# Layer 3's weighted sums in the scores' PSUM banks, earlier degrees, and the loads of layer 0 in a new order

## The chip, the cores and the metric

The kernel runs on one core of a Trainium2 chip, in one launch. The metric is the device time of the whole launch in microseconds. Before the change it is 3578.55 us, the median of 3 runs (3575.83 to 3585.26). The profiled execution has a span of 3568.9 us and a mean granted TensorE clock of 0.977.

## What is computed

There are 64 graphs of 256 nodes with 256 features, and a dense 256 x 256 adjacency matrix for each, all in fp32. Four layers follow each other, and each is `x = layernorm(x + layer(x, adj))`:

```
# layer 0: a recurrence over the nodes i = 0..255 (h starts as x)
x_par = sum_j (adj[j, i] / deg[i]) * h[j]
r, z  = sigmoid(x_i @ W_ioux.T + b + x_par @ W_iouh.T + b)
hc    = tanh(x_i @ W_coux.T + b + (x_par * r) @ W_couh.T + b)
h[i]  = z * x_par + (1 - z) * hc
# layer 1: relu(norm_adj @ (x @ W.T + b)), norm_adj = adj / sqrt(deg_i deg_j)
# layer 2: one attention head of width 256, mask = adj, relu on q, k, v and output
# layer 3: attention with 8 heads of width 32, masked where adj <= 0, output projection
```

Node i of the recurrence reads states of earlier nodes and, for the later nodes, x itself. So its 256 steps run one after the other, with all 64 graphs side by side. Layers 1 to 3 work on each graph by itself.

## The kernel before

**Setup of layer 0** (`_recurrence`, up to L714). The weights of the cell come first: four loads through `_load_wT` (L44), turned by TensorE transposes into WxT and WhT; then the biases, cut into three bf16 parts (L56), and small masks ("window", L149). A pool of their own holds these, and it is closed before the next one opens.

Then comes the part of the parents' sum that needs only x (L185 to L209): in eight groups of GB = 8 graphs, adj (A, two transfers from SyncE's queue) and x (Xs, two from ScalarE's) are loaded into two buffers each, GpSimd cuts A to a triangle (L195), TensorE multiplies (L172), ScalarE and VectorE copy the PSUM banks in turn (L208), and the sums go to Us in DRAM (L179).

After that follow, one after the other, the degrees of the first block of T = 32 nodes (`degrees(0)`, L267: four pieces of rows, each loaded and then reduced; then `dinv`), the adjacency block S, the first sums ACC from Us (L298), the masked block An (L464), and the first x (xq).

**The steps.** One step: the parents' sum xp is turned (L597), multiplied with WhT for r and z (L590), rx is turned and multiplied for the candidate, and VectorE makes the new state (L631). ScalarE copies the state to `hs` (L633), and two transfers put it into a ring of 64 nodes in SBUF, Hw (L640, `into_ring`). `flush` (L619) writes rows of the ring to Hd in DRAM: 32 at a time in each block, the last 16 after the last step (L855). The order of instructions in the steps is written by hand (`manual_schedule`). Loads that may wait go through `load_later`, which puts them in a queue by rank; two of them are begun in each of the first four steps of eight (L820).

**Layers 1 to 3** (`_layers`). When the recurrence is done, the weights, rows and columns of the three layers are loaded from ScalarE's queue (L877 to L884), W1 is turned, and a product of the values' bias with Wo is added to a bias row (L899). Then 64 graphs go through a pipeline written out by hand: `ROUND` (L1194) lists steps such as `B.qk2.0`; the letter says how many rounds ago the graph entered (L is the youngest, then A, B, C; E has layer 3's end), and each round begins with the loads of one new graph (L981).

PSUM has four banks under the tag "mm" (`bank`, L930), which every product and transposition takes in turn, and four banks "sc0" to "sc3" for the scores of layer 3 (L1126). The scores of one half of the heads (`s3`) fill the four "sc" banks; VectorE adds the mask (L1141), ScalarE takes the exponential (L1142), and GpSimd adds the two halves of the keys (p3s, L1144). `o3` (L1148) takes two "mm" banks, one for each half of the heads, and puts there the weighted sums (L1164) and the sums of the exponentials (L1155). `d3` (L1175) divides. `degrees_a` and `degrees_b` (L1001, L1012) make the inverse root of the degrees, `dis`, which `adT` (L1016) uses when it copies the turned adjacency.

Of the kernel before, what the change touches and what calls it, by code (L numbers as in the profile page):

```python
# [19 lines left out]
P = 128  # L20
# [50 lines left out]
def _recurrence(tc, ident, Hd, x, adj, W_ioux, b_ioux, W_iouh, b_iouh, W_coux, b_coux, W_couh, b_couh):  # L71
# [31 lines left out]
    with ExitStack() as ctx:  # L103
# [20 lines left out]
        with tc.tile_pool(name="r_setup", bufs=1) as tmp, tc.tile_pool(  # L124
            name="r_setup_ps", bufs=2, space=bass.MemoryType.PSUM
        ) as tps:
            for WT, wi, wc, s in ((WxT, W_ioux, W_coux, "x"), (WhT, W_iouh, W_couh, "h")):
                _load_wT(nc, tmp, tps, wi, ident, lambda c: WT[:, :, c % 2, c // 2 * 2, :], "i" + s)
                _load_wT(nc, tmp, tps, wc, ident, lambda c: WT[:, :, c, 1, :], "c" + s)
            bx, bh = (tmp.tile([1, 2, 3, P], F32, name=f"bias_{s}") for s in "xh")  # L130
            for t, bi, bc in ((bx, b_ioux, b_coux), (bh, b_iouh, b_couh)):
                for g in range(2):
                    nc.scalar.dma_start(
                        t[:, :, 2 * g, :],
                        bi[g * D:(g + 1) * D].rearrange("(c d) -> c d", c=2).unsqueeze(0),
                    )
                nc.scalar.dma_start(t[:, :, 1, :], bc.rearrange("(c d) -> c d", c=2).unsqueeze(0))
            nc.vector.tensor_add(bx, bx, bh)
            _split_bf16(nc, tmp, bias3, bx, "bias")

            span = tmp.tile([W, T // U, U], F32, name="span")
            nc.gpsimd.memset(span, 1.0)
            nc.gpsimd.affine_select(
                out=span, in_=span, pattern=[[U, T // U], [0, U]], compare_op=ALU.is_ge,
                fill=0.0, base=W - T // 2 - LAG - 1, channel_multiplier=-1,
            )
            for w in range(2):  # L149
                first = (w * T - W + T // 2) % W  # L150
                for lo, hi, at in ring(first, first + W):
                    for g in range(2):
                        nc.sync.dma_start(
                            window[w][g * W + at:g * W + at + hi - lo],
                            span[lo - first:hi - first].rearrange("p a u -> p (a u)"),
                        )
# [26 lines left out]


        with tc.tile_pool(name="r_first", bufs=2) as tmp, tc.tile_pool(  # L185
            name="r_first_ps", bufs=4, space=bass.MemoryType.PSUM
        ) as tps:
            for g in range(0, B, GB):
                A = tmp.tile([P, 2, GB, P], F32, tag="A", name=f"xA_{g}")
                Xs = tmp.tile([P, 2, GB, D], F32, tag="X", name=f"xX_{g}")  # L190
                for jc in range(2):
                    rows = slice(jc * P, (jc + 1) * P)
                    nc.sync.dma_start(A[:, jc], adj[g:g + GB, rows, 0:P].rearrange("b j i -> j b i"))
                    nc.scalar.dma_start(Xs[:, jc], x[g:g + GB, rows, :].rearrange("b j d -> j b d"))
                nc.gpsimd.tensor_mul(  # L195
                    A[:, 0], A[:, 0], tri.unsqueeze(1).to_broadcast([P, GB, P])
                )
                for n in range(0, GB, 4):
                    ub = tmp.tile([P, 4, D], F32, tag="ub", name=f"xu_{g}_{n}")
                    for e in range(0, 4, 2):  # L200
                        pb = tps.tile([P, 2, D], F32, tag="x", name=f"xp_{g}_{n}_{e}")
                        for q in range(2):
                            b = n + e + q
                            x_product(
                                pb, q, [A[:, jc, b, :] for jc in range(2)],
                                [Xs[:, jc, b, :] for jc in range(2)],
                            )
                        (nc.vector.tensor_copy if e else nc.scalar.copy)(ub[:, e:e + 2, :], pb)  # L208
                    x_out(0, g + n, ub)  # L209

        blk = ctx.enter_context(tc.tile_pool(name="r_blk", bufs=2))
        stream = ctx.enter_context(tc.tile_pool(name="r_stream", bufs=2))
        work = ctx.enter_context(tc.tile_pool(name="r_work", bufs=2))
        ps = ctx.enter_context(tc.tile_pool(name="r_ps", bufs=1, space=bass.MemoryType.PSUM))
# [24 lines left out]
        def load_later(out, in_, rank):  # L239

            begun = []

            def f(n):
                nc.sync.dma_start(out, in_)
                begun.append(n)

            loads.append((rank, f))
            loads.sort(key=lambda e: e[0])
            return begun
# [17 lines left out]
        def degrees(k):  # L267
# [16 lines left out]
            nc.vector.tensor_scalar(zero, deg, 0.0, None, ALU.is_equal)  # L284
            nc.vector.tensor_add(deg, deg, zero)
            nc.vector.reciprocal(deg, deg)
            nc.vector.tensor_scalar(zero, zero, -1.0, 1.0, ALU.mult, ALU.add)
            nc.vector.tensor_mul(deg, deg, zero)
            yield
            for h in range(2):  # L290
                at = k * T + h * HT
                for c in range(2):
                    nc.sync.dma_start(dinv[c * B:(c + 1) * B, at:at + HT], deg[h * B:(h + 1) * B])
# [69 lines left out]
        def early_load(e, got=[]):  # L363
# [5 lines left out]
            Hs = stream.tile([P, GB, D], F32, tag="Hs", name=f"Hs_{k}_{lo}_{t}", bufs=4)  # L369
# [267 lines left out]
        def into_ring():  # L637
            n, hs = ring_in.pop(0)
            for o in range(2):
                nc.sync.dma_start(Hw[n % W::W, :, o * P:(o + 1) * P], hs[o * B:(o + 1) * B])  # L640
# [19 lines left out]
        for _ in degrees(0):  # L660
            pass
        tables[0]["S"], double = load_S(0)
        double()
        tables[0]["Sd"] = chain_S(0)
        tables[0]["An"] = late_load(0)
        for a in range(3):
            sums_in(a)

        xq = {0: load_x(0)}
# [3 lines left out]
        xq[1] = load_x(1)  # L673
# [35 lines left out]
        for now in range(N):  # L709
# [9 lines left out]
            if n:  # L719
# [13 lines left out]
                if p > 3:  # L733
# [104 lines left out]
            if i == 24:  # L838
                flush(n - 8 - T, n - 8)
            early_ahead(n)  # L840
# [14 lines left out]
        flush(N - T // 2, N)  # L855


def _layers(tc, ident, Hd, Yd, x, adj, w1, b1, l2, l3, out):
# [8 lines left out]
    nc = tc.nc  # L867
    B, N, D = x.shape
# [5 lines left out]
    with ExitStack() as ctx:  # L874
        const = ctx.enter_context(tc.tile_pool(name="l_const", bufs=1))
        W1T = const.tile([P, 2, D], F32, name="W1T")
        W2 = {n: _load_w(nc, const, l2["W" + n], f"W2{n}") for n in "qkvo"}  # L877
        W3 = {n: _load_w(nc, const, l3["W" + n], f"W3{n}") for n in "qkvo"}
        b1_r = _load_row(nc, const, b1, "b1_r")
        b2_r = _load_row(nc, const, l2["bo"], "b2o_r")  # L880
        b3_r = _load_row(nc, const, l3["bo"], "b3o_r")
        cols = const.tile([P, 6, 2], F32, name="b_cols")
        for s, b in enumerate((l2["bq"], l2["bk"], l3["bq"], l3["bk"], l3["bv"], l2["bv"])):
            _load_col(nc, cols[:, s, :], b)  # L884
# [5 lines left out]
        with tc.tile_pool(name="l_setup", bufs=1) as tmp, tc.tile_pool(  # L890
            name="l_setup_ps", bufs=2, space=bass.MemoryType.PSUM
        ) as tps:
            _load_wT(nc, tmp, tps, w1, ident, lambda c: W1T[:, :, c * P:(c + 1) * P], "w1")

            bv = tmp.tile([P, 2, P], F32, name="bv3")
            nc.vector.tensor_copy(bv, cols[:, 4, :].unsqueeze(2).to_broadcast([P, 2, P]))
            pb = tps.tile([P, D], F32, tag="wt", name="bv3_ps")
            for k in range(2):
                nc.tensor.matmul(pb, bv[:, k, :], W3["o"][:, k, :], start=(k == 0), stop=(k == 1))  # L899
            nc.vector.tensor_add(b3_r, b3_r, pb)  # L900
# [5 lines left out]
        ctx.enter_context(tc.manual_schedule())  # L906
# [23 lines left out]
        def bank(name, shape=(P, 2, D)):  # L930
            return ps.tile(list(shape), F32, tag="mm", name=name, bufs=4)

# [40 lines left out]
        class Graph:  # L973
# [7 lines left out]
            def load(self):  # L981
                b = self.b
                self.y = io.tile([P, 2, D], F32, tag="y", name=f"y_{b}", bufs=7)
                nc.sync.dma_start(self.y, Hd[:, b, :].rearrange("(c p) d -> p c d", p=P))
# [3 lines left out]
                nc.sync.dma_start(self.ad, adj[b].rearrange("(c p) m -> p c m", p=P))  # L988

# [158 lines left out]
            def o3(self):  # L1148


                self.o_ps = [bank(f"o3_{self.b}_{hc}") for hc in range(2)]
# [43 lines left out]
            A.xT.1 B.xT.2 E.o3 E.d3.0 C.norm_b.2 E.d3.1 B.qk2.0  # L1195
            A.t B.qk2.1 B.v2 L.residual_0 B.masks
            E.f3 C.xT.3 A.g C.bias_3 L.norm_a.0
            C.qk3.0 C.qk3.1 E.norm_a.3 A.norm_a.1 L.norm_b.0 B.s2 B.exp2
            C.s3.0 C.v3 B.w2 L.degrees_a
            B.pT2 E.norm_b.3 E.store A.norm_b.1 C.s3.1 B.f2 L.degrees_b  # L1200
# [192 lines left out]
```

## Time and profile before

| Part of the trace | from to (us) | what is there |
|---|---|---|
| weights, masks | 0 to 21 | transposes of the cell's weights; DMA share 0.52, then 0.03 |
| x part of the sums | 21 to 122.6 | 8 groups; the last store to Us has landed at 122.6 |
| degrees, first loads | 122.6 to 152.8 | four loads and reductions of rows in turn, then dinv |
| 256 steps | 152.8 to 1563.1 | the last state is copied at 1562.83 to 1563.10 |
| passage to the layers | 1563.1 to 1595.2 | the last flush, then weights, then the first graph's loads |
| layers 1 to 3 | 1595.2 to 3569 | a new graph about every 30.0 us |

Over the whole span TensorE is busy 3223.1 us (90%), VectorE 2465.2 (69%), ScalarE 1900.3 (53%) and GpSimd 1874.5 (53%). These shares are means over stages with different limits, so the stages have to be read one by one: in a table of windows the columns are the busy time of TensorE, of its weight loads, of VectorE, ScalarE and GpSimd with the number of instructions, then the granted TensorE clock, the share of the 16 DMA engines, and GB/s. In the timeline and in the lists of groups, L1164 is line 1164 of the kernel, `a<-b` is output and inputs, and the bracket at the end has the idle time of the engine before the instruction and what ended it. TensorE's rows "x16" are instructions: an fp32 matmul is several of them.

### The profile page before, as it was taken

What the parts mean: (1) busy time and instruction counts of PE and PEld (TensorE: products, weight loads), DVE (VectorE), ACT (ScalarE), POOL (GpSimd) and SP (SyncE); (2) the same over time, 40 slices, a digit from 0 to 9 for tenths busy, and PEclk for the clock granted to TensorE, in tenths of its full rate; (3) what the DMA queues carried; (4) which work ended last, traced back from release to release, by engine and by line L of the source; (5) the groups of instructions that cost most, each with busy time, mean ns of one, the idle gap of its engine ahead of it and who ended that gap; (6) DMA issues with size and microseconds to landing.
All of it is one profiled execution on the core that took longest, in us unless ns stands there. A gap on an engine that the chain in (4) does not pass through costs nothing.

```text
span 3568.9 us, 80419 instructions
## 1 busy us (share of the span) xinstructions
PE 3223.1 (90%) x29350; PEld 2318.4 (65%) x29350; DVE 2465.2 (69%) x7052; ACT 1900.3 (53%) x5026; POOL 1874.5 (53%) x2181
## 2 busy tenths in 40 slices
PE   5599999999989898858999999999999999999998
PEld 4455555555555555536777777777777777777775
DVE  2366767767667777735777777777777777777776
ACT  0155545545445454424666666666666666666664
POOL 2266677767667778723444444444444444444443
PEclk9799999999999999978999999999999999999999
DMA  8846566787876564140111111111111111111100
GB/s 281 224 132 144 162 174 152 162 190 201 201 191 166 154 152 120 58 116 18 45 45 45 45 45 45 45 45 45 45 45 45 45 45 45 45 43 45 45 27 22
DMA packets 389637, 348.43 MB, mean 98 GB/s; under 512 B 107244, under 2 KB 355192, under 8 KB 384120
## 3 DMA queue, kind: packets, MB, share of 16 engines
q1 hardware_dynamic: 367280, 323.84, 34.0%
q10 hardware_dynamic: 21960, 19.41, 1.6%
q8 instruction: 235, 3.85, 0.4%
q14 instruction: 162, 1.33, 0.1%
HBM read 224.01 MB, written 99.61 MB: 91 GB/s over the span
## 4 chain that ended last, share of the span: by engine, by line
PE 61%; DVE 14%; DMA 6%; issue 6%; POOL 6%; ACT 5%; SPq 2%; ACTq 0%; DVEq 0%; POOLq 0%
PE mm L948 13%; PE rc L590 4%; DVE p L1141 4%; PE s L1132 4%; PE rc L582 3%; PE mm_g L948 3%; PE mm_t L948 3%; PE mm_3f L948 3%; PE mm_3v L948 3%; PE mm_2s L948 3%; PE mm_2v L948 3%; PE late L506 3%; DVE ACC L615 3%; PE mm_2w L948 3%; POOL ACC L651 2%
## 5 line engine op out<-in xcount | busy, mean ns | idle before, releaser
L615 DVE SCALAR_TENSOR_TENSOR ACC<-keep,S,ACC 128x128 f32<-128x128 f32 x1712 | 504.8, 345 | 187.4 <-ACT hs L633 170.0
L1144 POOL TENSOR_TENSOR p3s<-p 128x256 f32<-128x256 f32 x512 | 387.8, 788 | 329.6 <-ACT p L1142 329.3
L925 ACT ACTIVATE y<-y,shift,rstd 128x256 f32<-128x256 f32 x512 | 273.4, 593 | 303.9 <-DVE shift L923 259.9
L1044 POOL TENSOR_TENSOR y<-y,g 128x512 f32<-128x512 f32 x64 | 81.1, 1267 | 601.1 <-issue 590.2
L651 POOL TENSOR_TENSOR ACC<-ACC,far 128x384 f32<-128x384 f32 (+1 forms) x313 | 371.3, 1186 | 24.6
L582 PE MATMUL rc<-WxT,xqT 128*64 128x256 f32 x2048 | 326.3, 397 | 6.1 <-ACT lb L232 1.7
L1141 DVE TENSOR_TENSOR p<-s,neg 128x512 f32<-128x512 f32 x512 | 317.7, 683 | 10.9 <-PE s L1132 8.8
L755 POOL TENSOR_TENSOR ready<-ACC,dinv 128x128 f32<-128x128 f32 x255 | 101.9, 400 | 391.3 <-DVE ACC L615 372.4
L647 POOL TENSOR_TENSOR far<-hs,S 128x384 f32<-128x384 f32 (+1 forms) x313 | 304.3, 972 | 4.7
L1142 ACT ACTIVATE p<-p 128x512 f32<-128x512 f32 x512 | 294.6, 624 | 2.6 <-DVE p L1141 1.6
L913 DVE BATCH_NORM_STATS2 st<-y 128x6 f32<-128x256 f32 x512 | 209.0, 408 | 95.0 <-POOL y L1044 90.2
L917 POOL TENSOR_TENSOR rstd<-rstd,mhalf 128x2 f32<-128x2 f32 x256 | 173.6, 695 | 125.7 <-DVE rstd L916 122.2
L1178 DVE RECIPROCAL rT<-o 128x256 f32<-128x256 f32 x128 | 223.8, 1748 | 0.3 <-PE o L1155 0.2
L599 ACT COPY xpT<-xpT_ps 128x128 f32<-128x128 f32 x256 | 68.3, 267 | 254.9 <-PE xpT_ps L597 254.9
L1164 PE MATMUL o<-p,v 128*32 128x256 f32 x2048 | 138.4, 382 | 70.8 <-ACT xT L1030 70.8
L590 PE MATMUL rc<-WhT,xpT 128*64 128x128 f32 x2048 | 170.7, 288 | 28.8 <-ACT xpT L599 28.6
L590 PEld LDWEIGHTS rc<-WhT,xpT 128*64 128x64 f32 x2048 | 108.1, 137 | 118.6 <-ACT xpT L599 84.1
L1187 DVE TENSOR_TENSOR y<-y,mm_3f 128x512 f32<-128x512 f32 x64 | 44.0, 688 | 187.9 <-PE mm_3f L948 187.9
L582 PE MATMUL z_ps<-WxT,xqT 128*64 128x128 f32 x2048 | 170.0, 287 | 0.0
L1107 ACT ACTIVATE qk<-mm,b_cols 128x256 f32<-128x256 f32 x256 | 107.5, 471 | 115.9 <-PE mm L948 115.9
L506 PE MATMUL late<-Hw,An 64*32 64x256 f32 x3840 | 154.9, 389 | 9.3 <-issue 4.4
L815 DVE TENSOR_TENSOR zcc<-zc,rc 128x128 f32<-128x128 f32 x256 | 72.7, 284 | 130.0 <-ACT rc L813 129.3
(168 smaller groups left out, 8004.6 us busy)
## 6 DMA issues: line engine op xcount, KB each, us to landing
xX<-in_x_dram ACTq DMA_DIRECT2D x16, 1024.0 KB
Us<-xu SPq DMA_DIRECT2D x64, 256.0 KB
rows<-in_adj_dram SPq DMA_DIRECT2D x64, 256.0 KB
ACC<-Us SPq DMA_DIRECT2D x32, 512.0 KB
xq<-in_x_dram SPq DMA_DIRECT2D x64, 256.0 KB
Hw<-hs SPq DMA_DIRECT2D x512, 32.0 KB
Es<-eu SPq DMA_DIRECT2D x64, 256.0 KB
early_sb<-Es SPq DMA_DIRECT2D x32, 512.0 KB
```

Of the source, the lines that this page charges most:

```text
L506: nc.tensor.matmul(pb[g][q * T:(q + 1) * T, e, :], An[rows, b].rearrange("p u s -> p (u s)"), Hw[rows, b, :], start=True, stop=True,)
L582: nc.tensor.matmul(G[o * B:(o + 1) * B], xqT[a, i // 2][:, i % 2, kc, h * B:(h + 1) * B], WxT[:, kc, o, gates], start=False, stop=False, s ...
L590: nc.tensor.matmul(G[o * B:(o + 1) * B], hT[:, kc * B:(kc + 1) * B], WhT[:, kc, o, g], start=False, stop=(kc == 1), skip_group_check=True,)
L615: nc.vector.scalar_tensor_tensor(acc[:, 0, :], keep[:, j % 2, :], s, acc[:, 0, :], ALU.mult, ALU.add)
L647: nc.gpsimd.tensor_mul(tmp[:, 0:count, :], hs.unsqueeze(1).to_broadcast(shape), s.unsqueeze(2).to_broadcast(shape),)
L651: nc.gpsimd.tensor_add(acc, acc, tmp[:, 0:count, :])
L925: nc.scalar.activation(y[:, c, :], y[:, c, :], AF.Identity, bias=shift[:, c:c + 1], scale=rstd[:, c:c + 1],)
L948: nc.tensor.matmul(pm[:, c, :], lhsT[:, k, c * P:(c + 1) * P], rhs[:, k, :], start=(k == 0), stop=(k == 1),)
L1141: nc.vector.tensor_add(p, s_ps[i], self.neg3)
L1142: nc.scalar.activation(p, p, AF.Exp, scale=ISQ)
L1144: nc.gpsimd.tensor_add(both, p[:, 0, :], p[:, 1, :])
L1178: nc.vector.reciprocal(rT, o_ps[:, 1, :])
```

## The change

It has three parts, one for each of the places in the title.

*Layer 3's sums and the degrees.* `o3` takes the banks "sc0" and "sc1", where the scores of heads were, in place of two "mm" banks. In `ROUND` the degrees of the youngest graph are placed half a round earlier, so that `dis` is ready before `adT` asks for it, and the first product of layer 2, `B.qk2.0`, goes ahead of a normalization of another graph. The three loads of a graph come in the order x, adj, state.

*The setup of layer 0.* The loads of the first two groups of x and adj are the first transfers. The first degrees' rows come in one transfer for each half, and are reduced within the loop over the groups; the weights are loaded after the first group and turned after the fourth; all copies of the sums are VectorE's. x lies in buffers of a pool "wide", which is kept for the whole kernel, and which the steps use for earlier states.

*The passage to the layers.* The weights of the layers are loaded within the last 40 steps, through `load_later`, into three buffers of "wide". The states of the last eight steps go to Hd directly, not through the ring, and the ring's last flush is begun five steps before the end.

```diff
-        with tc.tile_pool(name="r_setup", bufs=1) as tmp, ...:
-            for WT, wi, wc, s in ((WxT, W_ioux, W_coux, "x"), (WhT, W_iouh, W_couh, "h")):
-                _load_wT(...)
+        first_in = [first_load(g) for g in (0, GB)]
+        rows_0 = fst.tile([P, T // 2, N], F32, name="rows_0", bufs=1)
+        for h in range(2):
+            nc.sync.dma_start(rows_0[h * B:(h + 1) * B], adj[:, h * T // 2:(h + 1) * T // 2, :])
...
             for g in range(0, B, GB):
-                A = tmp.tile(...)
-                Xs = tmp.tile(...)
+                A, Xs = first_in.pop(0)
...
-                        (nc.vector.tensor_copy if e else nc.scalar.copy)(ub[:, e:e + 2, :], pb)
+                        nc.vector.tensor_copy(ub[:, e:e + 2, :], pb)
                     x_out(0, g + n, ub)
+                if g + 2 * GB < B:
+                    first_in.append(first_load(g + 2 * GB))
+                if g == 0:
+                    load_weights()
+                if g == 3 * GB:
+                    turn_weights()
+                if g == 2 * GB:
+                    deg = fst.tile([P, T // 2], F32, name="deg_0", bufs=1)
+                    nc.vector.tensor_reduce(deg, rows_0, AX.X, ALU.add)
+                    inverse(deg, ...)
+                    dinv_from(deg, 0)
...
-        for _ in degrees(0):
-            pass
...
         def into_ring():
             n, hs = ring_in.pop(0)
             for o in range(2):
-                nc.sync.dma_start(Hw[n % W::W, :, o * P:(o + 1) * P], hs[o * B:(o + 1) * B])
+                to = Hw[n % W::W] if n < N - U else Hd[n]
+                nc.sync.dma_start(to[..., o * P:(o + 1) * P], hs[o * B:(o + 1) * B])
...
-                if p > 3:
+                if p > 3 or n >= N - U:
                     for _ in range(min(2, len(ring_in))):
                         into_ring()
...
+            if n == N - U + 3:
+                flush(N - T // 2, N - U)
+            if n == N - 5 * U:
+                then(lambda to, of: load_later(to, of, 3))
...
-        flush(N - T // 2, N)
...
             def load(self):
-                self.y = io.tile(...)
-                nc.sync.dma_start(self.y, Hd[:, b, :]...)
                 self.xin = ...
                 self.ad = ...
+                self.y = io.tile(...)
+                nc.sync.dma_start(self.y, Hd[:, b, :]...)
...
             def o3(self):
-                self.o_ps = [bank(f"o3_{self.b}_{hc}") for hc in range(2)]
+                self.o_ps = [
+                    ps.tile([P, 2, N], F32, tag=f"sc{hc}", name=f"o3_{self.b}_{hc}", bufs=1)
+                    for hc in range(2)
+                ]
...
         ROUND = """
-            A.xT.1 B.xT.2 E.o3 E.d3.0 C.norm_b.2 E.d3.1 B.qk2.0
-            A.t B.qk2.1 B.v2 L.residual_0 B.masks
-            E.f3 C.xT.3 A.g C.bias_3 L.norm_a.0
+            A.xT.1 B.xT.2 E.o3 E.d3.0 B.qk2.0 C.norm_b.2 E.d3.1
+            A.t B.qk2.1 B.v2 L.residual_0 B.masks L.degrees_a
+            E.f3 L.degrees_b C.xT.3 A.g C.bias_3 L.norm_a.0
             C.qk3.0 C.qk3.1 E.norm_a.3 A.norm_a.1 L.norm_b.0 B.s2 B.exp2
-            C.s3.0 C.v3 B.w2 L.degrees_a
-            B.pT2 E.norm_b.3 E.store A.norm_b.1 C.s3.1 B.f2 L.degrees_b
+            C.s3.0 C.v3 B.w2
+            B.pT2 E.norm_b.3 E.store A.norm_b.1 C.s3.1 B.f2
             L.adT B.norm_a.2
```

## The prediction

> **What bounds the kernel now.** I read the busy time by windows first. It shows three stages: setup up to 152.8 us (the first transpose of a step), 256 serial steps up to 1563.1, and layers 0 to 3 over 64 graphs up to 3569. Two windows:
>
> ```profile
> 80.00:90.00 10.00, 5.92 (x26) 4.51 (x25) 1.38 (x2) 1.17 (x2) 1.69 (x1) 0.97 1.12 364
> 1800.00:2400.00 600.00, 572.89 (x3920) 463.52 (x3919) 454.86 (x1141) 370.30 (x801) 275.40 (x340) 1.00 0.14 45
> ```
>
> The last column is GB/s, the one before it the DMA share, the one before that the granted TensorE clock. In setup the DMA engines are full (share 1.12, 364 GB/s) and TensorE is not. In the layers TensorE is busy 572.89 of 600 us at clock 1.00, so only its gaps can be won. Next, the chain of waits through setup, then through the passage from the last step to the first graph:
>
> ```profile
> 21.05 5.66 DMA xA<-in_adj_dram
> ...
> 119.79 2.52 DMA Us<-xu
> ...
> 123.18 4.20 DMA rows<-in_adj_dram
> ...
> 145.76 1.29 DVE deg L279 x2
> ...
> 149.83 0.59 SPq L293
> ```
>
> ```profile
> 1562.83 0.28 ACT hs L633
> ...
> 1566.64 10.37 DMA Hd<-Hw
> ...
> 1580.82 5.26 DMA W3o<-in_L_gnn_Wo_dram
> ...
> 1591.92 3.10 DMA xin<-in_x_dram
> 1595.18 1.27 POOL y L992
> ```
>
> Three idle stretches: 21 us before the big loads start, 30 us of small serial loads and reductions after them (122.6 to 152.8), and 32.1 us between the last state (1563.1) and the first residual (1595.2). Last, TensorE's waits in 1800 to 3400 (total us, times, longest), and one round of the timeline, 30.0 us long:
>
> ```profile
> PE o L1164 <- ACT xT L1030: 61.4, 53, 1.2
> PE o L1155 <- POOL p3s L1144: 9.1, 46, 0.2
> ```
>
> ```profile
> 2422.09 3.28 POOL L1144 TENSOR_TENSOR p3s<-p 128x256 f32<-128x256 f32 x4 [2.33 <-ACT p L1142]
> ...
> 2423.26 1.07 PE L1164 MATMUL o<-p,v 128*32 128x256 f32 x16
> 2423.33 0.69 DVE L1014 TENSOR_TENSOR dis<-dis,some 128x2 f32<-128x2 f32 x1
> 2424.12 0.84 ACT L1020 ACTIVATE adT<-tr_ad,dis 128x256 f32<-128x256 f32 x2 [0.62 <-DVE dis L1014]
> 2424.85 1.07 ACT L1030 COPY xT<-tr_x 128x512 f32<-128x512 f32 x2
> ...
> 2425.49 1.07 PE L1164 MATMUL o<-p,v 128*32 128x256 f32 x16 [1.15 <-ACT xT L1030]
> ...
> 2426.92 1.99 PE L948 MATMUL mm<-xT,W2q 128*128 128x256 f32 x8
> ```
>
> Nearly all of TensorE's idle time, 71 us in 53 rounds, sits here: the second half of layer 3's weighted sums takes a bank whose last reader is a copy (xT), which stands on ScalarE behind adT, which waits for the degrees (dis).
>
> [...]
>
> **Part 1: the layers' round.** No arithmetic goes or comes. The sums now use the banks of the scores' heads 0 and 1. Their last readers are the DVE adds p (end of all four 2421.9, in the built order the first two are what is waited for), and the next scores come 19 us later, after the divisions: nothing new waits. So the first half starts right after the transposes, at 2422.64 rather than 2422.84. The second half follows without its 1.15 us; the exponentials it needs ended at 2423.51. Work of both halves, from start to start of their rows: 0.42 + 0.87 and 0.89 + 0.43, 2.6 us, to 2425.2.
> What then ends last before W2q? Three candidates. TensorE itself, 2425.2 and the 0.33 to 0.41 "issue" gap that stands before such a change of tile: 2425.6. ScalarE: with degrees computed a half round earlier, adT follows the exponentials at once, 0.62 earlier, so the second xT ends at 2425.3. GpSimd: the fourth p3s ends at 2425.37; its sum (two rows, some 0.1 each) and the issue gap make 2425.8 to 2425.9. I take 2425.8: **1.1 us a round**. Bounds: 0.9 (p3s slips by 0.2) and 1.34 (all idle time, 71.3/53.3). Over 63 rounds: **69 us**, 57 to 84.
> The degrees move to where VectorE waits 3.0 us for mm_3f (L1187) and cost 0.68 + 3 x 0.17 there: hidden. GpSimd's power 0.70 lies in its idle time before y+g. W2q's relu now precedes norm_b of another graph on ScalarE; what waits for norm_b is xT.3, about 5 us later. mm_3f needs oT: VectorE's chain moves forward 0.6 with adT and ends at about 2431.2, mm_3f is due at 2432.6. All hidden. In a load, x and adj now go ahead of Hd on SyncE: worth nothing at a DMA share of 0.14.
>
> **Part 2: last step to first graph.** The weights (2.4 MB), rows and columns are loaded during the last 40 steps, 18 issues of about 0.5 us where the DMA share is 0.24 to 0.42 (windows from 1400 and 1500): hidden. The last eight states go straight to Hd, and the flush before them is issued five steps (24 us) before the end, against the 10.4 us that the flush took: hidden. What stays: last state 1563.1, two issues 1.06, landing 2.60, issue of y 0.38, landing 3.10, residual at about 1570.2 instead of 1595.2: 25 us. The first degrees no longer follow the norm (dis 1599.97 to 1601.9 sat between the norm and adT): 2 more. **27 us**, 23 to 30. W1's transposes and the bias product, some 4 us, run while that transfer lands.
>
> **Part 3: setup.** The big loads are first in their queues, so start at about 1 us instead of 21. But they are DMA-bound, and the weights (1.6 MB), rows of the first degrees (2.1) and S (0.6) now share the engines: 33.6 + 4.3 = 37.9 MB, at 365 GB/s 104 us. Added: 2.5 us start, 7 us for the last group's matmuls and stores (before: 113.1 to 122.6 at 208 and 144 GB/s), and about 3 for a bubble. In the built order VectorE reduces the rows (8 x 0.64, from L279's 128x512 reductions: 5 us) between the first two copies of group 0; behind it wait three copies, the stores of that group, and on SyncE the third group's adj load. Last store landed: about 116 us, not 122.6. Afterwards xq, ACC and raw still have to be loaded, since their buffers reuse the setup's: 2.6 MB, of which xq arrives after some 4 us; transposes to the first step take 4.6 (148.13 to 152.76). First step at about 124.5; with xq of block 1 loaded already (a 1.3 us wait in step 0), **29 us** saved, 20 to 38. The 30 us of degrees are inside the loop, where VectorE is busy 1 to 2 us in 10.
>
> The steps themselves keep their instructions and order. Sum: 69 + 27 + 29 = 125; 3578.55 - 125 = **3453 us**.
>
> **Rivals.**
> - *Another wait replaces the bank.* GpSimd and ScalarE end within 0.5 us of the new W2q; if p3s or xT slips, a round gains only 0.5: 32 + 27 + 29 = 88, **3490**. For: three chains end close together. Against: each is started by ACT or DVE work that the change does not delay.
> - *Setup stays full.* If rows, window and S block SyncE[...] and the adj loads come late, part 3 gives 10: **3472**. For: before, SyncE waited 31 us for TensorE at L193. Against: X, half of the bytes, is issued from ScalarE's queue.
> - *Slower.* A TensorE without gaps could be granted less: at 0.90, 28.65 us of work a round become 31.8, +1.8 x 63 = 113 less 56: **3635**. Against: the clock stays 1.00 at 95.5% busy, and the low values (0.50 to 0.86) stand where TensorE idles.
>
> **Chances.** Forecast 0.72, other wait 0.14, full setup 0.10, slower 0.04. Faster by over 0.3% in all but the last; 0.01 each is moved for mixtures: 0.95, 0.02, 0.03. Range: all high ends, 84 + 30 + 38 = 152, give 3426; the other wait's 3490 with 5 for its own spread gives 3495. I take 3424 to 3495.
>
> **What would show it.** Right: the round is 28.9 us (28.7 to 29.1), the row "o <- ACT xT" is gone from TensorE's waits, TensorE is busy some 99% in the layers; first residual about 7 us after the last state; first step at about 124 us with the last store at about 116. Wrong: a new row of 0.5 us or more a round before W2q (POOL p3s, ACT xT) or before mm_3f (DVE oT); the DMA share under 1 between 25 and 45 us; steps longer than before; a granted clock below 0.97 in the layers.

## The result, and the profile after

The changed kernel takes 3463.72 us (median of 4 runs, 3460.53 to 3467.76), the kernel before 3580.93 (4 runs): a ratio of 0.9674, 95% interval 0.9656 to 0.9692, or 117 us less. The forecast was 3453 and 125 us less. The two profiled executions differ by 105.2 us in span (3568.9 and 3463.7), because the one of before, at 3570.75 us, was 10 us under its median. By stages of these two:

| stage | before (us) | after (us) | difference | forecast |
|---|---|---|---|---|
| start to the first transpose of a step | 152.8 | 137.8 | -15.0 | -29 |
| from there to the last state | 1410.3 | 1416.2 | +5.8 | 0 |
| last state to the first store of layer 2's result (Yd) | 89.2 | 62.6 | -26.6 | -27 |
| 63 rounds, first to last of those stores | 1883.3 | 1812.2 | -71.1 | -69 |
| rest | 33.3 | 34.9 | +1.6 | 0 |

The layers and the passage came as forecast. The setup gave half, and the steps became a little longer.

**The layers.** The row of the table of windows (busy time of TensorE, of its weight loads, of VectorE, ScalarE, GpSimd; clock, DMA share, GB/s):

```profile
1700.00:2300.00 600.00, 600.00 (x4067) 484.84 (x4069) 482.94 (x1186) 383.76 (x834) 284.64 (x352) 1.00 0.14 46
```

TensorE is busy 600 of 600 us at clock 1.00; before it was 572.89. In TensorE's waits from 1700 to 3300 only one wait of 0.2 us is left; the row "o <- ACT xT" is gone. A round takes 28.77 us (1812.2 / 63) instead of 29.89. The ends of matmuls are modelled in this view, so 600 of 600 does not mean that nothing waits: busy time per round went from 28.54 us to 28.77 with the same work, and short waits of the weight loads are still there. The end of the weighted sums in one round of the timeline, with the lines that bound it:

```profile
2414.10 3.26 POOL L1195 TENSOR_TENSOR p3s<-p 128x256 f32<-128x256 f32 x4 [2.93 <-ACT p L1193]
...
2417.41 0.14 PEld L1209 LDWEIGHTS o<-p3s,ones 128*32 128x32 f32 x2 [0.33 <-POOL p3s L1195]
2417.95 1.59 PEld L999 LDWEIGHTS mm<-xT,weights 128*128 128x128 f32 x8 [0.41 <-issue]
```

The last sum's weight load waits 0.33 us for the fourth p3s, and W2q follows after the 0.41 us gap of a change of tile. This is the order that the prediction gave: GpSimd ends last, then the gap.

**The setup.** The chain of waits (start, length, what):

```profile
41.46 10.97 DMA xA<-in_adj_dram
...
124.96 2.52 DMA Us<-xu
...
130.25 6.73 DMA ACC<-Us
...
137.80 0.33 PE xpT_ps L614
```

The third group's adj is issued only at 41.46 us, the last store to Us lands at 127.5 (forecast 116), and the first step starts 10.3 us after that (forecast 8.5).

**The passage.** Chain, then the first residual in the timeline:

```profile
1553.68 0.28 ACT hs L650
...
1554.46 1.90 DMA Hd<-hs
```

```profile
1560.55 1.26 POOL L1043 TENSOR_TENSOR y<-y,xin 128x512 f32<-128x512 f32 x1 [7.54 <-DMA y<-Hd]
```

From the end of the last state to the first residual are 6.6 us; before they were 32.1, forecast were 7.

### The profile page after: what moved, and what is told of

The parts are those of the page before. It is cut to its first block, busy times and chain, and to the rows that moved or that the text cites. A ratio compares the mean times of both kernels' runs of the same rounds, so it can differ in the third digit from the quotient of the medians.

```text
span 3463.7 us, 80374 instructions
## 1 busy us (share of the span) xinstructions
PE 3228.6 (93%) x29350; PEld 2320.4 (67%) x29350; DVE 2502.0 (72%) x7061; ACT 1883.4 (54%) x5010; POOL 1873.9 (54%) x2181
## 4 chain that ended last, share of the span: by engine, by line
PE 73%; DVE 7%; DMA 7%; POOL 5%; issue 3%; ACT 2%; SPq 2%; ACTq 0%; DVEq 0%; POOLq 0%
PE mm L999 13%; PE rc L607 5%; PE s L1183 4%; PE rc L599 4%; PE mm_2f L999 4%; PE mm_3v L999 3%; PE mm_t L999 3%; PE mm_3f L999 3%; PE mm_2v L999 3%; PE mm_g L999 3%; PE mm_2s L999 3%; DVE ACC L632 3%; PE o L1218 3%; PE mm_2w L999 3%; PE late L523 3%
## 5 line engine op out<-in xcount | busy, mean ns | idle before, releaser
L999 PE MATMUL mm<-xT,weights 128*128 128x256 f32 x2048 | 481.9, 383 | 2.9 <-ACT xT L1081 2.9
L999 PEld LDWEIGHTS mm<-xT,weights 128*128 128x128 f32 x2048 | 384.8, 190 | 79.5 <-issue 25.5
L669 POOL TENSOR_TENSOR ACC<-ACC,far 128x384 f32<-128x384 f32 (+1 forms) x313 | 372.3, 1189 | 24.5
L1106 ACT ACTIVATE qk<-mm,weights 128x256 f32<-128x256 f32 x256 | 107.5, 471 | 268.0 <-PE mm L999 268.0
L951 DVE BATCH_NORM_STATS2 st<-y 128x6 f32<-128x256 f32 x512 | 208.8, 408 | 13.4 <-POOL y L1095 12.6
L1060 POOL TENSOR_TENSOR dis<-dis,mhalf 128x2 f32<-128x2 f32 x64 | 44.8, 700 | 277.0 <-DVE dis L1059 252.1
L212 PE MATMUL xp<-xX,xA 128*128 128x256 f32 x384 | 109.4, 423 | 66.3 <-POOL xA L685 39.5
L1158 ACT ACTIVATE qk<-mm,weights 128x256 f32<-128x256 f32 x256 | 107.5, 471 | 115.9 <-PE mm L999 115.9
```

Source lines behind the costliest of these rows:

```text
L669: nc.gpsimd.tensor_add(acc, acc, tmp[:, 0:count, :])
L951: nc.vector.bn_stats(st, y[:, c, :])
L999: nc.tensor.matmul(pm[:, c, :], lhsT[:, k, c * P:(c + 1) * P], rhs[:, k, :], start=(k == 0), stop=(k == 1),)
```

## The experiments

Times of single executions below are compared by stage, since the steps alone vary by some 15 us from one execution to another (shown further down). The setup varies too: in three profiles whose setup is the same (the kernel after, experiments 3 and 4) the last store to Us lands at 127.5, 126.3 and 129.1 us, and the first transpose of a step starts at 137.8, 136.6 and 139.3. A difference inside these ranges is not read as an effect.

**1 and 2. The bank and the order, each alone.** On the kernel before:

```diff
-                self.o_ps = [bank(f"o3_{self.b}_{hc}") for hc in range(2)]
+                self.o_ps = [ps.tile([P, 2, N], F32, tag=f"sc{hc}", ..., bufs=1) for hc in range(2)]
```

> The kernel before with one edit: layer 3's weighted sums take the banks of the scores' heads 0 and 1; the order of the round is the old one. Theory (the bank was the wait, the order a help): the second half of the sums no longer waits for xT, and W2q then waits for the second xT copy, which still stands behind the late degrees and ends at 2425.92 in the round shown, so W2q starts near 2426.0 instead of 2426.92: round 28.95 us instead of 29.89, 59 us less in all; a small new wait 'mm <- ACT xT' of 0.2 to 0.4 us a round. Rival (the order was the cause, the bank only its sign): W2q gains 0.6 or less, round 29.3 or longer, at most 38 us in all.

Measured: 3523.98 us, ratio 0.9855 (0.9832 to 0.9878); the round is 28.99 us (1826.1 / 63), so 0.91 us or 57 us in all. The end of the sums in its timeline:

```profile
2430.56 0.14 PEld L1158 LDWEIGHTS o<-p3s,ones 128*32 128x32 f32 x2 [0.55 <-POOL p3s L1144]
2431.11 0.94 PEld L948 LDWEIGHTS mm<-xT,W2q 128*128 128x128 f32 x5 [0.41 <-ACT xT L1030]
```

W2q now starts just after the second xT copy (2429.96 + 1.07 = 2431.03), which is late because adT still waits for the degrees. This is the bank theory, to 0.04 us a round.

The other half, also on the kernel before:

```diff
-            A.xT.1 B.xT.2 E.o3 E.d3.0 C.norm_b.2 E.d3.1 B.qk2.0
+            A.xT.1 B.xT.2 E.o3 E.d3.0 B.qk2.0 C.norm_b.2 E.d3.1
...                              (and degrees_a, degrees_b half a round sooner)
```

> The kernel before with one edit: the new order of the round (degrees placed sooner, W2q's relu ahead of the second norm); the sums stay in the shared banks. Theory (bank first): xT ends 0.62 us sooner since adT no longer waits for the degrees, so the wait 'o <- ACT xT' falls from 1.15 to about 0.5 us a round and the round from 29.89 to about 29.3, 39 us in all. Rival (order first): the wait falls under 0.1 us and the round reaches 28.8, some 69 us in all.

Measured: 3524.10 us, ratio 0.9849 (0.9833 to 0.9866); the round is 28.99 us (1826.2 / 63), the same 57 us. TensorE's waits from 1800 to 3400:

```profile
PE o L1164 <- ACT xT L1030: 13.0, 55, 0.4
PE o L1155 <- DVE f L1096: 10.4, 53, 0.2
```

Both expectations missed: 0.24 us of the wait for xT is left, where one theory said 0.5 and the other under 0.1. xT starts 1.10 us after the first sums (2403.30 against 2402.20) instead of 2.01 (2424.85 against 2422.84), so 0.9 sooner and not 0.62: besides the wait for the degrees, the exponentials stand earlier against the sums. The two halves of part 1 take away the same wait in two ways, so they don't add: 0.91 each, 1.13 together.

**3 and 4. The passage, each half undone in the kernel after.**

```diff
-                to = Hw[n % W::W] if n < N - U else Hd[n]
-                nc.sync.dma_start(to[..., o * P:(o + 1) * P], hs[...])
+                nc.sync.dma_start(Hw[n % W::W, :, o * P:(o + 1) * P], hs[...])
...
+        flush(N - T // 2, N)          # after the last state
```

> The kernel after with one edit undone: the last states go into the window Hw again and the last 16 are flushed to Hd after the last state, as before. Theory (the flush was a serial piece of the passage): the first residual starts 14 to 15 us after the last state instead of 6.6, since a flush of about 10.4 us (its row in the kernel before) takes the place of a store of about 2. Rival (the passage is held by something else, such as the W1 transposes or the x and adj loads): 6.6 to 8 us. The rest of the kernel as in the kernel after.

Measured: 20.0 us from the last state (1557.22) to the first residual, so 13.4 more, where 8 were expected. Its chain:

```profile
1561.01 10.36 DMA Hd<-Hw
...
1571.45 3.52 DMA xin<-in_x_dram
...
1577.25 1.26 POOL y L1040
```

The flush costs its 10.4 us, and x, adj and mhalf start only when it has landed, although none of them reads Hd. In the kernel after x and adj were issued at 1555.2 and 1555.7, right behind the last state's stores. That these tiles take over memory that Hw held would explain it; this was not tried by itself.

```diff
-                then(lambda to, of: load_later(to, of, 3))
...
+            then(lambda to, of: nc.sync.dma_start(to, of))   # after the last state
```

> The kernel after with one edit undone: the weights, rows and columns of layers 1 to 3 are loaded after the last state instead of within the last 40 steps. Theory 1 (their cost is their issue on SyncE, 18 issues of 0.5 us, and 2.4 MB at 365 GB/s beside it): the first residual starts about 16 us after the last state instead of 6.6. Theory 2 (few transfers are open at once, so that issues wait for landings): 20 to 25 us. Rival (x and adj and the state are what is waited for): under 8 us.

Measured: 17.9 us, so 11.3 more; theory 1 said 16, theory 2 20 to 25. About half of it is issue on SyncE, the rest waits near the end of the list:

```profile
1562.98 5.29 DMA weights<-in_L_gnn_bo_dram
...
1568.38 2.79 DMA xin<-in_x_dram
```

From 1557.70 to 1562.98 ten loads go out at 0.5 us each (theory 1); the small ones behind them wait for an earlier one to land, until 1568.4 (theory 2's effect, smaller than it said). The two halves add up: 13.4 + 11.3 = 24.7 of the 25.5 us of this stage, though the second is not quite the old state, in which ScalarE issued these loads.

**5 to 7. Why is the setup short of its forecast? The order of VectorE and SyncE.** In the kernel after VectorE makes the first copy at 15.35 us, then waits 13.6 us for the first degrees' rows, reduces them for 4.42, and makes the second copy at 34.02. SyncE's window loads stand from 12.1 to 32.2. Each was moved out of the way:

```diff
                 if g == 0:
+                    for h in range(2):
+                        nc.sync.dma_start(rows_0[h * B:(h + 1) * B], ...)    # no longer ahead of the loop
                     load_weights()
```

> The kernel after with the load of the first degrees' rows (rows_0) placed behind the first group's products, so that VectorE's reduction of them stands behind that group's four copies instead of between the first and the second. Theory A (the setup was short of the forecast because VectorE stood from 16.04 to 34.02 us waiting for those rows, and with it the first stores and, behind them on SyncE, the third group's adj load): that load starts before 30 us instead of 41.46, DMA moves over 300 GB/s from 20 to 50 us, the last Us store lands near 118 us instead of 127.5 and the first transpose of a step starts near 128 instead of 137.8. Theory B (the added small transfers make the DMA engines slower per byte, 329 GB/s instead of 365 at the same share, and SyncE waits for open transfers anyway): first transpose at 135 or later. Theory C (SyncE's window loads, which waited from 12 to 32 us for earlier transfers, are the block): 135 or later here, too, and the gain comes with the next kernel.

Measured: first transpose at 136.7 us, 1 us sooner and inside the range of the unchanged setup. All 64 matmul instructions of the first two groups (two for each fp32 matmul of the program here) now run without a break from 11.43 to 27.4, and then TensorE waits longer than before, for the third group's adj:

```profile
53.42 9.98 PE L210 MATMUL xp<-xX,xA 128*128 128x256 f32 x32 [26.03 <-DMA xA<-in_adj_dram]
```

```diff
+                if g == GB:
+                    for w in range(2): ...    # the eight window loads, no longer ahead of the loop
```

> The kernel after with only the eight window loads (1 KB to 6 KB) moved from the front of SyncE's queue to behind the second group; VectorE's reduction stays between the first two copies. Theory A: little, the first transpose of a step at 134 to 138 us, since the copies still wait for rows_0, which now may come a few us sooner. Theory B: 137. Theory C (the window loads block SyncE): 130 or sooner.

Measured: 140.0 us, 2 us later, just outside that range.

> Both edits, rows_0 and the window loads behind the first and the second group. Theory A: as with the rows alone or 1 to 3 us better, first transpose of a step at 126 to 128 us, total some 10 us below the kernel after (3454). Theory B: 135 or later, 3461. Theory C: like the windows alone, 130 or sooner.

Measured: 141.8 us, 4 us later; 3470.06 us in 5 runs, ratio 0.9688 (0.9673 to 0.9702), no better than the kernel after. Theories A and C fall: the bubble on VectorE and the block on SyncE are both there in the trace, but TensorE and VectorE have time to spare in this stage (busy 63 and 33 of the 113 us from 0.8 to 113.7), and filling their gaps moved the wait to the next transfer. Theory B came nearest: 135 or later in 5 and 7 came true, and in 6 it said 137. What makes the transfers slow is asked next.

**8. What the rows cost.**

```diff
-            nc.sync.dma_start(rows_0[h * B:(h + 1) * B], ...)
-                    nc.vector.tensor_reduce(deg, rows_0, AX.X, ALU.add)
+                    nc.vector.memset(deg, 128.0)
```

> The kernel after without the load and the reduction of the first degrees' rows (2.1 MB; the degrees of the first 32 nodes come from a constant, so the work that depends on them has other values). It prices that load in its place. Theory D (the setup is bound by the DMA engines, and these rows cost more than their bytes: 128 descriptors of 16 KB that took some 1.2 us each, 9.6 us of sixteen engines, 190 GB/s): the last Us store lands and the first transpose of a step starts 9 to 11 us sooner, the latter at 127 to 129 us. Theory B' (bytes at the usual 365 GB/s): 5 to 6 us sooner, 132. Theory E (SyncE's order and its open transfers set the pace, not the engines): under 3 us.

Measured: last store landed at 118.7, first transpose at 128.9 us, so 8.8 and 8.9 us sooner: near theory D, and more than the 5.7 us of 2.1 MB at 365 GB/s, though by little more than the range of the unchanged setup. The reading is not clean, since the order of the rest changed with it (TensorE first turned the weights and began the products only at 24.5).

**9, 10. Descriptors, and ScalarE's queue for adj.**

```diff
-        rows_0 = fst.tile([P, T // 2, N], ...)
+        rows_0 = fst.tile([P, T // 2, N + 8], ...)      # loads and reduction use [:, :, 0:N]
```

> The kernel after with the same rows in a tile whose rows are 264 instead of 256 columns long, so that each descriptor carries 1 KB instead of 16 KB; bytes, issues and order stay. Theory D (the long descriptors are slow): from 19 to 30 us DMA moves about 365 GB/s instead of 190, rows_0 lands 3 to 5 us sooner than 29.7, and the first transpose of a step starts 3 to 5 us sooner, near 134. Theory B' or E: no change of the rate, or a change that does not reach the end, 137 to 138.

Measured: first transpose at 137.2 us, no change, and the rate where the rows land is about as low as before. GB/s in 40 slices of 1.5 us from 0 to 60, first of the kernel after, then of this one:

```profile
GB/s 0 73 361 374 373 371 371 372 372 372 371 374 495 208 197 197 186 186 189 163 25 236 371 364 339 237 306 303 217 328 295 334 371 364 347 376 384 369 83 145
```

```profile
GB/s 0 90 358 371 370 374 372 371 373 371 374 370 378 267 223 190 218 197 192 150 1 55 291 366 290 319 312 345 288 140 320 369 371 372 372 388 384 386 239 180
```

From 19.5 to 30 us (slices 14 to 20) both move 150 to 270 GB/s, while the view's digits of the DMA share there are 8 and 9 tenths; a 1 KB descriptor of the rows takes about 90 ns in the trace, one of the x loads 46 (from 1 to 19 us). So the descriptor's length is not it.

```diff
-                nc.sync.dma_start(A[:, jc], adj[...])
+                nc.scalar.dma_start(A[:, jc], adj[...])
```

> The kernel after with the groups' adj loads issued from ScalarE, beside their x loads, instead of from SyncE, where they stand behind window loads, weights and the stores of the group before. Theory E (SyncE's order holds the third group's load to 41 us and leaves TensorE 15 us without work): the last Us store lands near 118 us and the first transpose is at 128 to 130. Theory D (the engines are the bound): the order moves work about, last store at 124 to 127, first transpose at 134 to 138.

Measured: last store landed at 128.5, first transpose at 139.0 us. TensorE's waits in the setup turn from adj (39.5 us for xA, as cut by GpSimd) to x (35.1 us for xX): theory E falls. Theory D's ranges were missed by a microsecond, which is inside the spread; that the engines are the bound fits, but is not shown by this run alone.

**11. The last small loads.**

```diff
-        xq = {a: load_x(a) for a in range(2)}
-        for a in range(3):
-            sums_in(a)
+        sums_in(0); xq = {0: load_x(0)}; sums_in(1); xq[1] = load_x(1); sums_in(2)
```

> The kernel after with another order of the last small loads: ACC of block 0, xq of block 0, ACC 1, xq 1, ACC 2, instead of both xq (four issues of 0.6 us) ahead of all three ACC. Theory: the first step's wait for ACC (landed at 137.0, 9.5 us after the last store) ends 3 to 4 us sooner, first transpose at 134 us. Rival (the transfers share the engines, so that the first lands no sooner): 137 to 138.

Measured: ACC arrives sooner and the first transpose starts at 131.8, but its copy stands on ScalarE behind those of xq, which now come later: the copy starts at 137.67 (137.1 to 139.9 with the setup unchanged) and that of the second step at 146.77 (143.1 to 146.1). Neither theory: the wait moved from ACC to xq, with nothing gained.

**12. Half of the partitions.** What the slow loads have in common, with 16 KB and 1 KB descriptors alike, is their destination: partitions 0 to 63, then 64 to 127. The same bytes on every second partition:

```diff
-            nc.sync.dma_start(rows_0[h * B:(h + 1) * B], adj[...])
+            nc.sync.dma_start(rows_0[h::2], adj[...])
...
+                half = deg[h * B:(h + 1) * B] if k else deg[h::2]
```

> The kernel after with the two loads of the first degrees' rows laid on every second partition (half h on partitions h, h+2, ...) instead of on partitions 0 to 63 and 64 to 127, and the store of the first degrees read back likewise; bytes, descriptors of 16 KB and order stay. Theory F (a transfer that fills one half of the partitions writes at half the rate: 190 to 200 GB/s with 16 KB and with 1 KB descriptors alike): from 19 to 30 us DMA moves over 300 GB/s, rows_0 lands 3 to 5 us sooner than 29.7 and the first transpose of a step starts 3 to 4 us sooner, near 134. Rival G (the source sets the rate, 64 rows 256 KB apart in DRAM): 190 to 220 GB/s as before, first transpose at 137 to 138. Total in either case within the spread of the loop, 3460 to 3468.

Measured: a 16 KB descriptor of these loads takes 0.61 us instead of 1.23 (median in the trace). VectorE's reduction, first of the kernel after, then of this one:

```profile
29.69 4.42 DVE L708 TENSOR_REDUCE deg<-rows 128x16 f32<-128x4096 f32 x1 [13.65 <-DMA rows<-in_adj_dram]
```

```profile
24.67 4.42 DVE L709 TENSOR_REDUCE deg<-rows 128x16 f32<-128x4096 f32 x1 [8.60 <-DMA rows<-in_adj_dram]
```

In the windows the DMA share from 19.5 to 24 us, when the rows move, is the same in both, and the last column, GB/s, doubles:

```profile
19.50:24.00 4.50, 2.33 (x11) 1.71 (x9) 0.00 (x0) 0.00 (x0) 0.00 (x0) 0.98 0.95 200
```

```profile
19.50:24.00 4.50, 2.69 (x13) 2.03 (x11) 0.00 (x0) 0.00 (x0) 0.00 (x0) 1.00 0.94 393
```

The reduction starts 5.0 us sooner, the last store lands at 121.1 instead of 127.5, and the first transpose starts at 130.9 instead of 137.8: 6.9 us (5.6 to 8.4 against the three unchanged setups), more than theory F said. In no other kernel with these rows did the last store land before 126.2. Rival G (the source's pitch) falls, since the source is the same. The total, 3461.94 us (4 runs; ratio 0.9662, 0.9635 to 0.9689), can't be told from the kernel after's 0.9674; the gain is shown in the stage, not in the total.

## Why the prediction was right, and where it was not

**Part 1, 69 us forecast, 71 measured: right.** Round 28.9 forecast (1.1 off one round of 30.0; the mean round was 29.89), 28.77 measured; the wait on xT went, TensorE has hardly a gap, and GpSimd's last p3s ends the sums as named. The degrees lie in VectorE's idle time, and no new wait came before mm_3f. The rival "another wait replaces the bank" (0.5 us a round) did not come: p3s costs 0.33 us and was in the forecast. The clock stayed at 1.00 with TensorE full, so "slower", whose 0.90 was the author's assumption, did not come either.

**Part 2, 27 forecast, 26.6 measured: right.** Experiments 3 and 4 split it: the flush 13.4, the weights 11.3. The prediction took the flush at its 10.4 alone and did not see that it also held up loads that don't depend on it; the sum came right because the whole stretch was read from the chain.

**Part 3, 29 forecast, 15 measured: the step that failed.** The mechanism held: the big loads go first, the stage is bound by DMA, and the degrees' serial loads are gone from behind it. What failed is the term "37.9 MB, at 365 GB/s 104 us". The loads of x and adj into 128 partitions did run at about that rate: 361 to 374 GB/s in the slices from 3 to 18 us of the kernel after (first list of experiment 9), and 323 to 369, stores to Us among them, in the eight windows of 10 us from 30 to 110 of the kernel before. But from the first load to the last packet of x the mean rate was 312 GB/s in the kernel after and 329 in experiment 12 (last column):

```profile
0.80:113.70 112.90, 63.04 (x244) 50.40 (x245) 33.44 (x55) 0.00 (x0) 24.48 (x15) 0.85 1.03 312
```

```profile
0.80:107.90 107.10, 69.80 (x237) 53.96 (x238) 35.36 (x55) 0.00 (x0) 25.64 (x16) 0.81 1.03 329
```

The 2.1 MB of rows came at some 190 GB/s, and with each half spread over every second partition they gave back 6.9 of the missing 13.3 us (experiment 12). Their bytes alone explain 5.3 of these (2.1 MB at 190 instead of 365 GB/s); the rest is within the spread. In the kernel after, where each half goes to 64 neighbouring partitions, the six slices from 19.5 to 28.5 us show 186 to 208 GB/s. The prediction took one rate for all loads. The "bubble" of 3 us was the wrong place to look: VectorE stood for 18 us, and taking that away gave 1 us, no more than the spread (experiment 5). The prediction's own sign of trouble here, a DMA share under 1 between 25 and 45 us, did come (0.95, 246 GB/s). Of the rest, 1.8 us lie between the last store and the first step (10.3 instead of 8.5). About 5 us remain between 121.1 and the forecast 116; the slices under 300 GB/s, where the small transfers of S, the windows and the weights pass, are where they would be, but no run took these apart. The rival "setup stays full" came nearer in size (10, measured 15) but had another cause: SyncE's order, which was tried in 6, 7 and 10 and gave nothing.

**"The steps keep their instructions and order": 0 forecast, +6 measured.** From the first to the last copy of xpT the three profiles with the old steps take 1405.0, 1405.4 and 1409.3 us, the eleven with the new 1405.0 to 1419.6, mean 1414.0. So some 7 us are likely the change's, though single executions overlap. Longer steps were among the prediction's own signs of being wrong. The largest piece is step 126, on average 2.8 us longer: 5.3 to 7.2 us with the old kernel's steps, 6.3 to 11.6 with the new one's. GpSimd's waits there, first of the kernel before, then of the kernel after:

```profile
POOL ACC L827 <- DMA late_sb<-Lb: 4.9, 1, 4.9
```

```profile
POOL ACC L878 <- DMA late_sb<-Lb: 9.2, 1, 9.2
```

A late sum's way through DRAM and back ends last in both. The kernel after is the longest of its eleven here. Why it takes longer after the change is open; it was not tried.

So the forecast of 3453 was 11 us low. Setup (14), steps (6) and rest (2), less the layers' 2, make 20 us by the profiled executions; some 10 of them do not show in the total, because the profiled execution of before was 10 us faster than its median.

**Two readings that were off without effect.** The last stage is layers 1 to 3, not 0 to 3. And low clocks do not stand only where TensorE idles: in the kernel before it was busy 4.79 of the 5 us from 100 to 105 at a clock of 0.50. The clock was 0.50 from 1570 to 1610, too, where TensorE was busy 11.4 of the 40 us; eight mm_t rows took 3.78 us there (1603.39) and 1.89 at a clock of 1.00 (2428.75).

## What to carry to other kernels

When a copy or sum waits for a buffer, look for a tile whose last reader is long done, and place the producers of the last waiter sooner: either took away most of the wait here (0.91 us a round each, 1.13 together), so price them together and not as a sum. Where the DMA engines were full (share 1.03 from 0.8 to 113.7 us), filling an engine's gaps gave nothing (first transpose 1 us sooner, 2 and 4 us later in experiments 5 to 7); price each transfer by the rate at which its own kind runs (361 to 374 GB/s for x and adj, some 190 for the rows), and look at which partitions its destination covers before counting its bytes: 64 neighbouring ones took twice as long as every second one here (1.23 against 0.61 us for 16 KB). In experiment 3 a late store also held back loads that don't read it (13.4 us for a flush of 10.4).

## What was not expected of the hardware

The loads of 1 MB into 64 neighbouring partitions ran at some 190 GB/s with the engines shown as busy (a share of 0.91 from 19.5 to 30 us), whether their descriptors carried 16 KB (1.23 us each) or 1 KB (about 90 ns each, where those of the x loads into 128 partitions took 46); on every second partition a 16 KB descriptor took 0.61 us. The DMA share did not tell these apart (0.95 at 200 GB/s, 0.94 at 393 from 19.5 to 24 us); the GB/s column did.
